# A graph layer's opening: later adjacency loads and gate weights fetched behind the last table write, one product moved behind a transpose, rows normalized a step later

## The chip, the cores and the metric

The kernel runs on one core of a Trainium2 chip. The metric is the device time of one execution in microseconds, the median of several. A profiled execution has its own time; the profile's times count from the first instruction of the span.

## What is computed

Two graph layers on x (3327 x 256, float32) with a sparse 0/1 adjacency adj (3327 x 3327, about four ones in a row), each followed by a residual and a layer norm. The change lies in layer 0, a graph attention whose result goes through a gated recurrent cell:

```python
Wh = h @ W                                   # h is x
e = leaky_relu(Wh @ a[:F] + (Wh @ a[F:]).T, 0.2)
att = softmax(where(adj > 0, e, -9e15), axis=1)
h_prime = att @ Wh
gi = h_prime @ w_ih.T + b_ih                 # i_r, i_z, i_n
gh = h @ w_hh.T + b_hh                       # h_r, h_z, h_n
r, z = sigmoid(i_r + h_r), sigmoid(i_z + h_z)
n = tanh(i_n + r * h_n)
x1 = layernorm(x + (1 - z) * n + z * h)
```

Layer 1 takes x1, builds a dense top-p attention (queries, keys, sorting by thresholds, two steps) beside a walk over adj, and gives the output. It takes most of the time and is not changed.

## The kernel before

Rows are handled in 26 tiles of 128 (NT; the last has 127). Layer 0 never forms the dense attention: it finds the ones of each adj row, gathers the neighbours' rows of Wh from a table in DRAM, and sums them with weights.

**Projection.** `run` first loops over t, the 26 tiles. `project` transposes x on PE (L753), copies on ACT (L754), multiplies by W (L758), copies the result into one of six `table` buffers (L762) and writes it on ACT's DMA queue to the DRAM table `whx` (L763 and L764, the DMA itself in the helper `move_rows`, L102). The next tile's transpose and L754 are issued ahead of this tile's L758 to L764. ACT's queue also carries, between these writes, the loads of adj tiles 1 and 2 (L1084, at t = 4 and 10) and of the gates' weights `whh` and `wih` (L1087, at t = 15 and 17). `totals` closes the stage: a maximum over all tiles and the mean row, written to the table as its last row (L794); `tell_src` splits scores into bfloat16 parts (L776 to L779).

**Searching.** `neighbours` is a generator of five steps for a tile of adj: four `max_index` searches (L819, one for each quarter of the columns, on DVE) and a step of small operations (L824 to L832). It also asks for the load of the adj tile three further on, on SP's queue (L822), since three buffers (`array`) rotate. `find` does one step. Each load goes in two parts, the first three quarters and the last.

**The pipeline of tiles.** `advance` is one phase: some `find` steps, then, every sixth phase (EVERY = 6), the start of a new tile; then each open tile, oldest first, issues its next step; then one step of `first_logits`, which starts layer 1's first scores once all searches are done. Phase 6t + s thus holds step s of tile t. A phase isn't a barrier: PE, ACT, DVE and POOL issue in the order of the program, and each runs on as far as its own waits let it.

```python
        engines = {
            mybir.EngineType.PE, mybir.EngineType.Activation, mybir.EngineType.DVE, mybir.EngineType.Pool,
        }
        with self.tc.manual_schedule(engines=engines):
```

SP is not in the set. [...]

The steps of a tile that matter here:

| step | what | engine, line |
|---|---|---|
| 0 to 2 | degree, its prefix sum `pst` | DVE L851, POOL L858 to L872, PE L865 |
| 4, 7 | mid, y; mem | ACT L875 to L878; DVE L884 |
| 6 | tell | POOL L880, L881 |
| 10, 12 | pe; ei, erow | PE L889, ACT L893 |
| 13 | which, hit, k | DVE L898 to L906 |
| 14 to 17 | edge list; five gathers from `whx`; src, e | POOL L908, L613, L918, L921 |
| 20, 21 | squares | ACT L927 |
| 22 | e | DVE L929 to L931 |
| 23 to 25 | five exponents | ACT L936 |
| 26 | weighted sum acc | PE L940 |
| 28, 29 | rs; h; pn's product of x | DVE L943, ACT L947, PE L950 and L953 |
| 30 | prz's product of x; transposes ph of h | PE L956 and L958, L961 |
| 31 | hT | ACT L964 |
| 33, 34 | products of hT | PE L967, L972 |
| 35 to 38 | gates, n, row statistics | ACT L978, L987; DVE L981 to L994 |
| 39 | power, shift | POOL L996 to L999 |
| 40 | normalized row, its write to `x1_rows` | ACT L1001, L102 |
| 41 on | query and key: ptq, xtq, pq, qT, kT | `qk`, PE L626, L636, ACT L629, L643, L644 |

From t = 13 (EARLY) the projection loop calls `advance` itself, so phases 0 to 12 lie in it; the other phases follow `totals`. The searches in a phase are `min(1, phase % 3)` in the loop, one from phase 13 to 23, and then FINDS = (0, 0, 0, 2, 1, 2) by the phase's place in the six.

Of the kernel before, what the change touches and what calls it, by code (L numbers as in the profile page):

```python
# [9 lines left out]
F32 = mybir.dt.float32  # L10
# [6 lines left out]
P = 128  # L17
N = 3327
D = 256
DC = D // P  # L20
DA = 64
NT = (N + P - 1) // P
# [35 lines left out]
EVERY = 6  # L58

EARLY = 13  # L60

FINDS = (0, 0, 0, 2, 1, 2)
# [19 lines left out]
def rows(t):  # L82
    return TAIL if t == NT - 1 else P


def cols(t):
    return slice(t * P, t * P + rows(t))
# [9 lines left out]
def move_rows(engine, dst, src, r):  # L97

    full = r // 16 * 16
    for a, b in ((0, full), (full, r)):  # L100
        if a < b:
            engine.dma_start(dst[a:b], src[a:b])  # L102
# [545 lines left out]
class Layer0:  # L648
# [165 lines left out]
    def neighbours(self, t):  # L814

        nc, r, ad = self.nc, rows(t), self.ad[t % 3]
        at = self.st.tile([P, SEG, 8], U32, tag="at8", name=f"at8_{t}")
        for g in range(SEG):
            nc.vector.max_index(at[:r, g, :], self.ones8[:r], ad[:r, g, :])  # L819
            yield  # L820
        if t + 3 < NT:
            self.load_adj(t + 3, nc.sync)  # L822
        off = self.st.tile([P, SEG, 8], F32, tag="off", name=f"off{t}")
        nc.vector.tensor_tensor(off[:r], self.base[:r], at[:r], ALU.subtract)  # L824
        key = self.key[:r, t]
        nc.vector.scalar_tensor_tensor(key, at[:r], SW - 0.5, off[:r], ALU.is_lt, ALU.mult)
        info = self.info[:, t]
        flat = key.rearrange("p g e -> p (g e)")
        nc.vector.max(info[:r, :8], flat)
        rest = self.st.tile([P, SEG * 8], F32, tag="rest", name=f"rest{t}")  # L830
        nc.vector.match_replace(rest[:r], info[:r, :8], flat, 0.0)
        nc.vector.max(info[:r, 8:16], rest[:r])  # L832
        yield

    def tile(self, t):

        nc, r, sh = self.nc, rows(t), self.sh
# [4 lines left out]
        def to(step):  # L842
            nonlocal done
            while done < step:
                done += 1
                yield
# [70 lines left out]
        src = self.small("src", f"src{t}", EB)  # L917
# [12 lines left out]
        nc.vector.scalar_tensor_tensor(e, e, ALPHA, e, ALU.mult, ALU.max)  # L930
        nc.vector.tensor_tensor(e[:, 0, :], e[:, 0, :], e[:, 1, :], ALU.subtract)  # L931

        for step, ks in ((23, (0, 1)), (24, (2, 3)), (25, (4,))):
            yield from to(step)
            for k in ks:
                nc.scalar.activation(ms[k], ms[k], AF.Exp, bias=e[:, 0, k : k + 1], scale=-FAR)  # L936
# [12 lines left out]
        ones3 = self.ones3[:, :r]  # L949
        nc.tensor.matmul(pn[:r], ones3, self.bias[:, 2 * D :], start=True, stop=False)  # L950
        xs = [self.xT[:, c, cols(t)] for c in range(DC)]
        for c in range(DC):
            nc.tensor.matmul(pn[:r, :D], xs[c], self.whh[:, c, 2 * D :], start=False, stop=False)  # L953
        yield from to(30)
        prz = self.ps1.tile([P, 2 * D], F32, tag="prz", name=f"prz{t}")
        nc.tensor.matmul(prz[:r], ones3, self.bias[:, : 2 * D], start=True, stop=False)  # L956
        for c in range(DC):
            nc.tensor.matmul(prz[:r], xs[c], self.whh[:, c, : 2 * D], start=False, stop=False)  # L958
        ph = self.ps.tile([P, DC, P], F32, tag="tr", name=f"ph{t}")
        for c in range(DC):  # L960
            nc.tensor.transpose(ph[:, c, :r], h[:r, c * P : (c + 1) * P], sh.ident[:r, :r])  # L961
        yield from to(31)
        hT = self.work.tile([P, DC, P], F32, tag="hT", name=f"hT{t}")
        nc.scalar.copy(hT[:, :, :r], ph[:, :, :r])  # L964
        yield from to(33)
        for c in range(DC):
            nc.tensor.matmul(  # L967
# [29 lines left out]
        nc.gpsimd.tensor_tensor(mv[:r, 1:2], mv[:r, 1:2], self.power[:r], ALU.pow)  # L997
        shift = self.small("shift", f"shift{t}")
        nc.gpsimd.tensor_scalar(shift[:r], mv[:r, 0:1], mv[:r, 1:2], -1.0, ALU.mult, ALU.mult)  # L999
        yield from to(40)  # L1000
        nc.scalar.activation(x1, x1, AF.Identity, bias=shift[:r], scale=mv[:r, 1:2])  # L1001
        move_rows(nc.scalar, sh.x1_rows[t * P : t * P + r, :], x1, r)
        yield from to(41)
        yield from sh.qk(self.ps, self.work, 0, t, x1, "tr")

    def erow(self, t):
# [28 lines left out]
    def run(self):  # L1035
        nc, sh = self.nc, self.sh
        self.load_adj(0, nc.sync)
        parts = self.st.tile([P, 4, DC], F32, tag="parts", name="parts", bufs=1)
        cuts = (0, 8, 16, NT - 2, NT)
        tiles, finding = [], iter(())  # L1040
        found = phase = 0
        self.done, self.searched = 0, False
        logits = self.first_logits()

        def find():

            nonlocal finding, found
            if next(finding, True):
                if found < NT:
                    finding = self.neighbours(found)  # L1050
                    found += 1
                    next(finding)
                else:
                    self.searched = True

        def advance(finds):
            nonlocal phase
            for _ in range(finds):
                find()
            if phase % EVERY == 0 and phase // EVERY < NT:  # L1060
                tiles.append(self.tile(phase // EVERY))
            for g in list(tiles):
                if next(g, True):
                    tiles.remove(g)
                    self.done += 1
            next(logits, None)
            phase += 1
# [5 lines that stand above are left out]
            self.weights()  # L1073
            opened = [self.project(t) for t in range(NT)]
            qk_weights = sh.make_weights(self.work, self.ps)
            pc = self.ps1.tile([1, 512], F32, tag="acc", name="colsum")
            next(opened[0])
            for t in range(NT):
                if t + 1 < NT:
                    next(opened[t + 1])  # L1080
                for _ in opened[t]:
                    pass
                if t in (4, 10):
                    self.load_adj(1 + t // 10, nc.scalar)  # L1084
                if t in (15, 17):
                    w, src = ((self.whh, self.wih)[t // 17], self.gates[t // 17])
                    nc.scalar.dma_start(w, src.rearrange("(c p) d -> p c d", p=P))  # L1087
                if t in (8, 10):
                    next(qk_weights)
                if t + 1 in cuts:  # L1090
                    k = cuts.index(t + 1) - 1
                    self.column_sums(parts[:, k, :], cuts[k], cuts[k + 1])
                if t - 1 in cuts[1:]:
                    k = cuts.index(t - 1) - 1
                    self.mean_terms(pc, parts[:, k, :], k == 0, False)
                if t == EARLY:
                    self.tell_src(0, EARLY)
                if t >= EARLY:
                    advance(min(1, phase % 3))
                elif t >= EARLY - 8:  # L1100
                    find()
            self.totals(pc, parts[:, 3, :])
            self.tell_src(EARLY, NT)
            while phase < EVERY * NT or tiles:
                advance(1 if phase < 4 * EVERY else FINDS[phase % EVERY])
            for _ in logits:
                pass
        full = self.st.tile([P, 3], F32, tag="full", name="full")

        nc.vector.tensor_reduce(full[:, 0:1], self.key.rearrange("p t g e -> p (t g) e")[:, :, 7], AX.X, ALU.max)  # L1110
        nc.vector.tensor_reduce(full[:, 1:2], self.info[:, :, MAXDEG - 1], AX.X, ALU.max)
        end = self.st.tile([P, NT], F32, tag="e0", name="end", bufs=1)
        nc.vector.scalar_tensor_tensor(end, self.deg, 1.0, self.info[:, :, MAXDEG], ALU.max, ALU.add)
        nc.vector.tensor_reduce(full[:, 2:3], end, AX.X, ALU.max)
        nc.vector.tensor_scalar(full[:, 2:3], full[:, 2:3], -float(EB * P), None, ALU.add)
        nc.vector.tensor_reduce(full[:, 0:1], full, AX.X, ALU.max)
        nc.vector.tensor_scalar(sh.bad[:, 0:1], full[:, 0:1], 0.5, None, ALU.is_gt)
        nc.vector.tensor_scalar(sh.rinv, self.deg, 1.0, None, ALU.add)
        nc.vector.reciprocal(sh.rinv, sh.rinv)
# [860 lines left out]
```

## Time and profile before

| what | value |
|---|---|
| median of 3 runs | 1857.93 us (1853.77 to 1858.95) |
| profiled execution, its own time | 1861.15 us |
| its span | 1859.1 us |
| PE, DVE, POOL, ACT busy over the span | 1666.4, 1318.3, 1158.7, 1031.2 us |
| last table write issued | 63.65 us, the mean row 65.52 us |
| first edge list (L908), last one | 68.33 us, 353.40 us |
| last normalization of layer 0 (L1001) | 394.86 us |

Lines of the profile are read so: start and length in us, engine, line of the kernel, operation, what is written from what. In brackets is the idle time before it and what ended it. A row of waits has who waited for whom, the us in total, how often and the longest. A row of a stretch has the busy us of PE, PE's weight loads, DVE, ACT and POOL, each with its number of instructions, then the granted TensorE clock (1 is full), the mean busy share of the DMA engines and GB/s. "q" behind an engine is its queue, which issues DMAs.

### The profile page before, as it was taken

What the parts mean: (1) busy time and instruction counts of PE and PEld (TensorE: products, weight loads), DVE (VectorE), ACT (ScalarE), POOL (GpSimd) and SP (SyncE); (2) the same over time, 40 slices, a digit from 0 to 9 for tenths busy, and PEclk for the clock granted to TensorE, in tenths of its full rate; (3) what the DMA queues carried; (4) which work ended last, traced back from release to release, by engine and by line L of the source; (5) the groups of instructions that cost most, each with busy time, mean ns of one, the idle gap of its engine ahead of it and who ended that gap; (6) DMA issues with size and microseconds to landing.
All of it is one profiled execution on the core that took longest, in us unless ns stands there. A gap on an engine that the chain in (4) does not pass through costs nothing. (4 is left out here: it accounts for less than half of the span.)

```text
span 1859.1 us, 27521 instructions
## 1 busy us (share of the span) xinstructions
PE 1666.4 (90%) x8093; PEld 1221.4 (66%) x8093; DVE 1318.3 (71%) x4095; ACT 1031.2 (55%) x2373; POOL 1158.7 (62%) x1908
## 2 busy tenths in 40 slices
PE   6589999969999999999996999999999988679994
PEld 4355555547777777777774777777777656568873
DVE  5688888456555665655546999999999876585872
ACT  2356666735556555555653555555555446676563
POOL 1578888637886666666654655666666573455754
PEclk9799998979999999999997999999999998889997
DMA  9766664212221111111101111111111120122330
GB/s 313 229 230 212 212 209 119 70 58 76 83 63 43 41 41 40 44 49 46 43 26 40 46 46 49 49 53 55 51 52 49 49 61 20 40 77 89 120 97 29
DMA packets 95099, 154.22 MB, mean 83 GB/s; under 512 B 16471, under 2 KB 68174, under 8 KB 94941
## 3 DMA queue, kind: packets, MB, share of 16 engines
q1 hardware_dynamic: 63818, 86.51, 14.2%
q0 software_dynamic: 20384, 53.28, 11.0%
q10 hardware_dynamic: 10738, 12.58, 2.1%
q8 instruction: 67, 1.10, 0.3%
q14 instruction: 92, 0.75, 0.1%
HBM read 124.65 MB, written 27.75 MB: 82 GB/s over the span
## 5 line engine op out<-in xcount | busy, mean ns | idle before, releaser
L1419 PE MATMUL pav<-xa,at 128*128 128x256 f32 (+2 forms) x1352 | 333.0, 391 | 8.8 <-ACT at L1405 8.8
L1405 ACT COPY at<-pt 128x512 f32<-128x512 f32 (+2 forms) x364 | 192.0, 542 | 262.7 <-PE pt L1403 168.3
L1419 PE MATMUL pav<-x,at 128*128 128x256 f32 (+2 forms) x1352 | 325.7, 385 | 7.9 <-ACT at L1405 7.6
L1419 PEld LDWEIGHTS pav<-xa,at 128*128 128x128 f32 (+2 forms) x1352 | 247.1, 192 | 90.0 <-ACT at L1405 41.8
L1419 PEld LDWEIGHTS pav<-x,at 128*128 128x128 f32 (+2 forms) x1352 | 244.4, 190 | 72.6 <-ACT at L1405 28.5
L1199 ACT COPY array<-pl 128x416 f32<-128x416 f32 (+4 forms) x405 | 183.1, 503 | 182.8 <-PE pl L1196 179.5
L1212 DVE MAX8 cand<-array 128x8 f32<-128x167 f32 (+5 forms) x921 | 239.0, 335 | 48.5 <-ACT array L1199 48.5
L613 POOL DMA_INDIRECT g<-xf_rows,edge x130 | 136.1, 1047 | 160.0 <-PE pxf L1365 127.9
L613 POOL DMA_INDIRECT g<-x_rows,edge x130 | 146.1, 1124 | 103.6 <-PE ptq L626 70.9
L1196 PE MATMUL pl<-kT,qT 64*128 64x416 f32 (+4 forms) x810 | 198.7, 561 | 6.3 <-ACT x L1584 2.7
L1304 DVE TENSOR_TENSOR_SCAN before<-e 128x40 f32<-128x40 f32 (+3 forms) x52 | 14.5, 279 | 227.0 <-ACT e L1297 217.7
L1357 POOL TENSOR_SCALAR m<-col,erow 128x128 f32<-128x128 f32 x260 | 157.0, 618 | 14.4 <-PE pxf L1365 8.0
L613 POOL DMA_INDIRECT g<-whx,edge x130 | 137.6, 1058 | 43.6 <-issue 35.6
L1365 PE MATMUL pxf<-g,m 128*128 128x256 f32 (+1 forms) x520 | 134.7, 408 | 13.2 <-POOL m L1357 6.4
L1365 PEld LDWEIGHTS pxf<-g,m 128*128 128x128 f32 (+1 forms) x520 | 98.6, 199 | 68.8 <-issue 40.7
L1230 DVE MAX8 lst<-cand 128x8 f32<-128x160 f32 (+3 forms) x364 | 114.6, 315 | 9.2 <-issue 0.2
L1403 PE MATMUL pt<-ident,array 128*128 128x128 f32 (+1 forms) x676 | 100.9, 276 | 6.0 <-DVE array L1320 6.0
L819 DVE FIND_INDEX8 at<-ones,array 128x8 uint32<-128x840 f32 (+1 forms) x104 | 105.6, 1027 | 0.0
L1403 PE MATMUL pt<-ident,p 128*128 128x128 f32 (+2 forms) x676 | 100.3, 274 | 4.3 <-DVE p L1320 4.3
L1403 PEld LDWEIGHTS pt<-ident,array 128*128 128x128 f32 (+1 forms) x676 | 84.9, 144 | 24.2 <-PE pxf L1365 7.6
L1403 PEld LDWEIGHTS pt<-ident,p 128*128 128x128 f32 (+2 forms) x676 | 84.7, 144 | 21.6 <-PE pxf L1365 8.0
L1320 DVE SCALAR_TENSOR_TENSOR array<-array,t,array 128x3327 f32<-128x3327 f32 x26 | 96.2, 3699 | 0.5
(467 smaller groups left out, 3321.6 us busy)
## 6 DMA issues: line engine op xcount, KB each, us to landing
array<-in_adj_dram SPq DMA_DIRECT2D x23, 1248.0 KB
array<-in_adj_dram SPq DMA_DIRECT2D x23, 415.5 KB
xf_rows<-xf SPq DMA_DIRECT2D x50, 128.0 KB
xa_rows<-xa SPq DMA_DIRECT2D x50, 128.0 KB
xfs<-xf_rows SPq DMA_DIRECT2D x50, 128.0 KB
whx<-table ACTq DMA_DIRECT2D x25, 129.5 KB
x_rows<-x ACTq DMA_DIRECT2D x25, 128.0 KB
xb_rows<-xb SPq DMA_DIRECT2D x25, 128.0 KB
```

The costliest lines, as they stand in the source:

```text
L613: self.nc.gpsimd.indirect_dma_start(out=dst[:, b, :], out_offset=None, in_=table[:, :], in_offset=bass.IndirectOffsetOnAxis(ap=self.edge[: ...
L819: nc.vector.max_index(at[:r, g, :], self.ones8[:r], ad[:r, g, :])
L1196: nc.tensor.matmul(pl[:r, :w], q[on], self.sh.kT[on, n, s : s + w], start=True, stop=True)
L1199: nc.scalar.copy(l[:r, h * HALF + s : h * HALF + s + w], pl[:r, :w])
L1212: self.nc.vector.max(cand[:r, g * 8 : g * 8 + 8], src[:r, g * group : min(N, (g + 1) * group)])
L1230: nc.vector.max(lst[:r, k : k + 8], cand[:r])
L1320: nc.vector.scalar_tensor_tensor(v.p[:r], v.l[:r, :N], v.t[:r], v.p[:r], ALU.is_ge, ALU.mult, accum_out=sA[:r])
L1357: nc.gpsimd.tensor_scalar(v.m[:, b, :], sh.col1, sh.erow[:, v.at, b : b + 1], None, ALU.is_equal)
L1365: nc.tensor.matmul(acc[:r, :D], v.m[:, b, :r], v.g[:, b, :], start=(b == 0), stop=(b == EB - 1))
L1403: nc.tensor.transpose(pt[: rows(j), j - j0, :r], v.p[:r, cols(j)], self.ident[:r, :r])
L1405: nc.scalar.copy(at[:, :full, :r], pt[:, :full, :r])
L1419: nc.tensor.matmul(v.acc[: v.r, :D], at[:k, j - 4 * g, : v.r], V[:k, j, :], start=(j == 0), stop=(j == NT - 1))
```

## The change

1. `neighbours` no longer loads the adj tile three further on but puts its number on a list `wanted`; `advance` takes one number a phase from it once the phase is past NT - EARLY = 13, and then loads it on SP's queue.
2. Adj tiles 1 and 2 are loaded on ACT's queue at t = 6 and 13 instead of 4 and 10.
3. The gates' weights are loaded behind `totals`, that is behind the last table write, on ACT's queue.
4. Searches: from t = 4 instead of 5; in the loop every second phase instead of two in three; none in phases 13 to 15; two a phase in 16 to 23.
5. The exponents go in two groups (steps 24 and 25) instead of three (23, 24, 25).
6. prz's bias and product of x are issued in step 31 behind the copy hT, not in step 30 ahead of the transposes ph.
7. The normalization and its write move from step 40 to 41, and `qk` from 41 to 42.

```diff
@@ neighbours
         if t + 3 < NT:
-            self.load_adj(t + 3, nc.sync)
+            self.wanted.append(t + 3)
@@ tile
-        for step, ks in ((23, (0, 1)), (24, (2, 3)), (25, (4,))):
+        for step, ks in ((24, (0, 1, 2)), (25, (3, 4))):
...
         yield from to(30)
-        prz = self.ps1.tile([P, 2 * D], F32, tag="prz", name=f"prz{t}")
-        nc.tensor.matmul(prz[:r], ones3, self.bias[:, : 2 * D], start=True, stop=False)
-        for c in range(DC):
-            nc.tensor.matmul(prz[:r], xs[c], self.whh[:, c, : 2 * D], start=False, stop=False)
         ph = self.ps.tile([P, DC, P], F32, tag="tr", name=f"ph{t}")
...
         nc.scalar.copy(hT[:, :, :r], ph[:, :, :r])
+        prz = self.ps1.tile([P, 2 * D], F32, tag="prz", name=f"prz{t}")
+        nc.tensor.matmul(prz[:r], ones3, self.bias[:, : 2 * D], start=True, stop=False)
+        for c in range(DC):
+            nc.tensor.matmul(prz[:r], xs[c], self.whh[:, c, : 2 * D], start=False, stop=False)
         yield from to(33)
...
-        yield from to(40)
+        yield from to(41)
         nc.scalar.activation(x1, x1, AF.Identity, bias=shift[:r], scale=mv[:r, 1:2])
         move_rows(nc.scalar, sh.x1_rows[t * P : t * P + r, :], x1, r)
-        yield from to(41)
+        yield from to(42)
@@ run
-        self.done, self.searched = 0, False
+        self.done, self.searched, self.wanted = 0, False, []
@@ advance
             for _ in range(finds):
                 find()
+            if self.wanted and phase > NT - EARLY:
+                self.load_adj(self.wanted.pop(0), nc.sync)
@@ run
-                if t in (4, 10):
-                    self.load_adj(1 + t // 10, nc.scalar)
-                if t in (15, 17):
-                    w, src = ((self.whh, self.wih)[t // 17], self.gates[t // 17])
-                    nc.scalar.dma_start(w, src.rearrange("(c p) d -> p c d", p=P))
+                if t in (6, 13):
+                    self.load_adj(1 + t // 13, nc.scalar)
...
                 if t >= EARLY:
-                    advance(min(1, phase % 3))
-                elif t >= EARLY - 8:
+                    advance(min(1, phase % 2))
+                elif t >= EARLY - 9:
                     find()
             self.totals(pc, parts[:, 3, :])
+            for w, src in zip((self.whh, self.wih), self.gates):
+                nc.scalar.dma_start(w, src.rearrange("(c p) d -> p c d", p=P))
             self.tell_src(EARLY, NT)
             while phase < EVERY * NT or tiles:
-                advance(1 if phase < 4 * EVERY else FINDS[phase % EVERY])
+                advance(FINDS[phase % EVERY] if phase >= 4 * EVERY else 2 if phase >= 16 else 0)
```

## The prediction

> **What bounds the kernel now.** I read the cores row (1859.1 us, one core), then stretches of time, because all edits lie in layer 0, which ends near 400 us; behind it the program is the same. First the stretches of the opening (busy us of PE, PEld, DVE, ACT, POOL; granted clock; DMA share; GB/s):
>
> ```profile
> 28.00:34.00 6.00, 3.53 (x20) 2.50 (x18) 5.35 (x16) 0.75 (x2) 0.31 (x2) 1.00 1.06 291
> 34.00:40.00 6.00, 2.31 (x8) 1.79 (x9) 0.38 (x3) 1.62 (x5) 0.37 (x2) 0.74 1.04 398
> 40.00:46.00 6.00, 5.85 (x22) 4.40 (x21) 4.94 (x15) 1.92 (x6) 1.67 (x10) 0.69 1.01 392
> 58.00:64.00 6.00, 4.91 (x29) 2.61 (x28) 3.97 (x13) 2.88 (x8) 0.98 (x6) 1.00 0.61 184
> 70.00:80.00 10.00, 0.52 (x11) 0.45 (x11) 9.17 (x30) 2.78 (x10) 7.84 (x18) 0.50 0.92 333
> ```
>
> All DMA engines are full to about 60 us while PE and ACT idle: the projection waits for transfers. ACT's waits from 12 to 66 us say which:
>
> ```profile
> ACT xT L754 <- DMA whx<-table: 6.0, 4, 3.9
> ACT xT L754 <- DMA array<-in_adj_dram: 5.7, 3, 3.7
> ```
>
> The table write is in front of that copy in ACT's queue, and it waits 11.7 us for older transfers. Then the order of the adj loads (DVE, SP, ACT, in three answers of the timeline):
>
> ```profile
> 32.78 1.03 DVE L819 FIND_INDEX8 at<-ones,array 128x8 uint32<-128x840 f32 x1
> ...
> 33.84 0.37 SPq L102 DMA_DIRECT2D array<-in_adj_dram  x1
> ...
> 45.33 0.33 ACTq L102 DMA_DIRECT2D whx<-table  x1
> 45.80 0.39 ACTq L1087 DMA_DIRECT2D whh<-in_whhT_dram  x1
> ```
>
> The load of adj tile 4 is called for behind the write at 45.33, but leaves at 33.84, 30 ns after the third search of tile 1 (32.78 + 1.03) freed its buffer. SP isn't in the ordered engine set; its place in the code doesn't hold it back.
>
> Then a tile in the steady part, on POOL and on DVE:
>
> ```profile
> 202.78 0.20 POOL L908 TENSOR_SCALAR edge<-k 128x5 uint32<-128x5 f32 x1
> ...
> 211.05 1.01 POOL L613 DMA_INDIRECT g<-whx,edge  x1 [0.31 <-issue]
> 212.09 0.21 POOL L918 TENSOR_TENSOR src<-ei 128x5 f32<-128x5 f32 x1
> 212.41 0.76 POOL L921 TENSOR_SCALAR e<-src,dmax 128x5 f32<-128x5 f32 x1
> 213.13 0.43 POOL L880 CAST tell<-info 128x1 bf16<-128x1 f32 x1
> ...
> 214.53 0.20 POOL L908 TENSOR_SCALAR edge<-k 128x5 uint32<-128x5 f32 x1
> ...
> 212.17 0.54 DVE L884 TENSOR_SCALAR mem<-y,square 128x640 bf16<-128x640 f32 x1
> 212.63 0.42 DVE L989 SCALAR_TENSOR_TENSOR n<-rz,n 128x256 f32<-128x256 f32 x1
> 213.09 0.42 DVE L990 TENSOR_TENSOR x<-x,n 128x256 f32<-128x256 f32 x1
> ```
>
> From the first edge list at 68.33 POOL's queue runs without a hole but the 0.3 us of issue behind each gather. It sets 9.8 us a tile first, 11.75 us for the 18 tiles from 108.9 to 320.3. After 354 the last tiles leave every 9.27 us (h at 361.03, 370.30, 379.56), with PE busy without a gap. So what counts is when POOL starts, its time per tile, and PE's sum in the drain.
>
> **The change part by part.** The sum is against the profiled execution (1861.15 us, span 1859.1), 3.2 us above the median of 1857.93; I take the difference off the median.
>
> Transfers in the opening. Adj loads 1 and 2 stay on ACT's queue, two and three projections later; both gate weights (1.57 MB) leave the stage. Loads 3 and 4 are called for at phases 14 and 15, but by the row above they leave once their buffers are searched, near 25 and 35 us, still inside the stage. From 24 us on before the last write: adj 1 to 4 (6.65 MB), half of adj 5 (0.8), 19 writes (2.5): 10 MB at 340 GB/s (mean of the six stretches 22 to 58) is 29 us: 53. The engines alone: write of tile 6 at 23.84, 7 tiles at 1.3 us (17.76, 18.85, 20.18) and 12 at 1.5 (49.79 to 63.28 for tiles 17 to 25 is 13.5/9) end at 51. The same count for before (12.6 MB from 20.5) gives 57.5, where the DMAs fall quiet near 60.5, 3 us later; with fewer loads colliding I add under half of that: last write at 54.7 instead of 63.28, **-8.6**. The transfers still here (adj 3 beside 1, 4 beside 2) leave ACT waits of 2 to 4 us.
>
> Searches (1.03 us each, the fifth step 1.3 of small operations). Before: 16 steps by phase 12, one a phase to 23, 27 in all. After: 15, none in 13 to 15, two a phase from 16, 31 in all. The first edge list loses the search at 66.33 that stands before it in DVE's queue: **-1.0**. DVE then has between the lists of tiles 0 and 1 8 steps, 8.6 us, plus 1.8 of others: 10.4, where POOL takes 10.8. Between those of tiles 1 and 2: 8 more, 11.1 us with e, mem and k, where POOL takes 9.8: what is late there is `which` L898, POOL behind it: 1.3 less the 0.4 in hand, **+0.9**. This needs adj 3 to 5 landed, which the early SP loads give. Gates behind the mean row: 4.6 us at 340 GB/s from about 57; first used at phase 29 (89.4 now, 21 us behind the first edge list); 0. If ACT must wait for an older transfer to issue them, its next work (mid, phase 16) has 3 us; without cover, that wait counts in full.
>
> Normalization (L1001) a step later, its x1_rows DMA with it. ACT waits 43.6 us for POOL's shift in 16 tiles from 125 to 310, with mid, y, rz, h queued behind. All of it lies beside POOL's full queue, so the wait itself is worth 0. The two later users move too: ptq (PE) now stands beside ph, 0 while PE has time to spare (busy 37.6 of 40 us from 200 to 240, so 0.7 us a tile); without it what it waits counts in full. In the drain a phase is no time; the last norm may stand behind a logits copy (0.91): 0 to +1.
>
> prz's x product behind h's transposes: the same five PE instructions. hT's copy comes 2.3 us sooner (prz bias 0.38, x 1.98), where POOL (steady) and PE's sum (drain) set the end: 0. Exponents in two groups (3, 2) instead of three: the same five at 0.4, all still ahead of the product at step 26; 0. The searches end four steps sooner, so two logit pairs (0.97 each) leave the drain: -2 to 0. I take 0 for norm and logits together.
>
> POOL's time per tile. With the norm out of mid's way I expect k, L884, L989 and L990 up to 1 us earlier against POOL. Rows: e and tell take 1.24 us from start to start (212.41 to 213.65) beside these three, but 0.55 (87.45 to 88.00) in tile 1 without them: 0.69 lost each tile. Moved earlier they lie on the fifth gather and on src. The Trainium skill (SBUF — State Buffer, Who interferes with whom) says that a DVE operation in a two-port mode, or with two SBUF inputs, takes a port pair that GpSimd shares, for the whole instruction, and that descriptor generation starves likewise. By it nearly all of the loss would move along (L884's 0.54 to the gather, 0.2 to src): 0. The trace is milder: the gather at 95.91 beside L884 took 1.33 against 1.00 (one at 76.17 only 1.10), so +0.33, +0.2, -0.69: -0.2 a tile, 18 tiles **-3.6**. I take the trace; the ends are -0.6 (all freed: -11) and +0.3 (L985 or L990 on two more POOL operations: +5).
>
> Sum: -8.6 - 1.0 + 0.9 - 3.6 = -12.3; by the rule -8.7. Predicted 1857.93 - 12.3 = 1845.6, about 1846.
>
> **The rivals.** *The likeliest* (0.50): start 8 to 9 us earlier, tile slightly shorter; own range 1840 to 1852. *POOL freed* (0.15): 0.6 less per tile, -8.7 - 11: 1838. For it: nothing but the lock lengthens those two rows. Against: five gathers leave POOL few moments when DVE is harmless. *The lock lands worse* (0.14): +0.3 a tile, -8.7 + 5: 1854. *The opening moves less* (0.13): the change does not do what it says, as SP's loads keep their time, the 11.7 us of ACT waits return behind adj 3 and 4; only the gates' 4.6 us and the search's 1.0 are won, less 0.9 and with no gain per tile: 1853.
>
> *Slower* (0.08): one mechanism, the searches at the head of DVE's queue. If loads 3 to 5 do wait behind the last write, they start with the gates at 52 us: 6.6 MB. At the 144 GB/s of the stretch from 80 to 90 that is 46 us, adj 5 at 98; five steps and tile 6's first follow, near 109 with adj 6, and tile 2's edge list behind them in DVE's queue comes 20 us after its old 88.92: less some 3 won later, 1875. At the 333 GB/s of the stretch from 70 to 80 adj 5 lands at 72 and nothing is lost. It decides where adj 5 lands after about 79. Against it: that stretch had nothing else to move, and SP isn't held.
>
> **How the numbers follow.** What this kernel's measurement can tell from no change is about 0.3%, 5.6 us: faster is under 1852.4. The likeliest and the freed case lie there (0.65), of the two small ones half (0.13): 0.78. The other half, same: 0.13. Slower, with a little of the worse lock: 0.09. The range 1834 to 1856 takes in the ends of the time per tile and leaves out the slow case.
>
> **What would show it.** First L908 near 58.5 (56 to 62) instead of 68.33; adj 3 leaving SP near 25, far ahead of the last table write; the ACT waits on transfers 11.7 down to 2 to 4; L908 to L908 11.75 down to 11.4 to 11.7, by e and tell shorter than 0.76 and 0.43; the wait of L1001 for L999 gone without a gain of its own; h every 9.27 us at the end. I am wrong if POOL waits long for k, if first edge lists stay past 64, or if the gain sits after 400 us.

## The result and the profile after

| what | before | after |
|---|---|---|
| median of 11 runs each | 1858.00 us (1853.77 to 1859.08) | 1849.76 us (1846.67 to 1854.28) |
| span of the profiled execution, its clock | 1859.1 us, 0.951 | 1846.6 us, 0.960 |
| last table write, mean row issued | 63.65, 65.52 us | 63.26, 65.14 us |
| first edge list (L908) | 68.33 us | 66.95 us |
| L908 to L908, steady tiles | 11.75 us | 11.25 us |
| last normalization of layer 0 (L1001) | 394.86 us | 385.01 us |

The ratio after to before is 0.9958, 95% interval 0.9948 to 0.9967. Of the profiled span's 12.5 us, layer 0 holds 9.9; the rest is in layer 1, which is the same program and takes 1461.6 us in this execution and 1464.2 in before's. In the thirteen profiled executions of this document it takes from 1458.9 to 1467.4, so these 2.6 us are within what executions differ by.

First the stretches of the opening, of after (columns as before: PE, PEld, DVE, ACT, POOL; granted clock; DMA share; GB/s):

```profile
28.00:34.00 6.00, 6.00 (x33) 4.13 (x31) 4.80 (x17) 2.32 (x7) 0.56 (x3) 1.00 1.03 396
52.00:58.00 6.00, 1.80 (x16) 1.20 (x16) 2.64 (x7) 1.25 (x6) 0.37 (x2) 0.77 0.92 315
58.00:64.00 6.00, 5.43 (x15) 2.85 (x16) 1.17 (x5) 2.06 (x6) 1.11 (x7) 0.66 0.18 56
```

The projection runs without a gap from 28 to 34 us. But in the stretch from 52 to 58 PE idles beside full DMA engines, and in the next it is busy at a clock of 0.66. The hole has moved, not gone. ACT's waits of after from 12 to 66 us:

```profile
ACT mid L875 <- DMA array<-in_adj_dram: 3.9, 1, 3.9
...
ACT xT L754 <- DMA whx<-table: 3.1, 1, 3.1
...
ACT xT L754 <- DMA array<-in_adj_dram: 2.2, 1, 2.2
```

That is 9.2 us of the old 11.7. (The 3.1 stands beside the load of adj 1, which ACT's own queue issues from 21.98 on, for 2.63 us.) The longest of them in SP's, ACT's and PE's timelines of after; SP's first row is adj tile 3:

```profile
25.02 3.54 SPq L102 DMA_DIRECT2D array<-in_adj_dram  x2
...
50.08 1.80 SPq L102 DMA_DIRECT2D array<-in_adj_dram  x2
```

```profile
53.46 0.38 ACT L762 COPY table<-pw 128x258 f32<-128x258 f32 x1 [0.50 <-PE pw L758]
57.31 0.33 ACTq L102 DMA_DIRECT2D whx<-table  x1
57.69 0.26 ACT L875 ACTIVATE mid<-pst,half 128x1 f32<-128x1 f32 x1 [3.85 <-DMA array<-in_adj_dram]
```

```profile
52.24 1.14 PE L758 MATMUL pw<-W_sb,xT 128*128 128x258 f32 x4 [0.29 <-ACT table L762]
...
58.05 2.09 PE L758 MATMUL pw<-W_sb,xT 128*128 128x258 f32 x4 [3.50 <-ACT info L876]
```

Adj tile 5 leaves SP at 50.08, among the last table writes. The write of tile 23 is ready at 53.84, leaves at 57.31, and mid, which stands behind it in ACT's queue, is put down to the adj load. The write doesn't read that load's data. I read the row as a link between the two queues: the write had to wait until that load had landed. SP's adj loads wait for table writes too, with which they share no data: 30.3 us in five waits in before, from 12 to 66 us. What links them (in my reading a semaphore for landed transfers that the program gives to DMAs of both queues in turn) no run shows. Full DMA engines alone are not enough: in before adj 5 leaves at 49.36, with a DMA share of 1.01 from 52 to 58, and no table write behind it waits. PE pauses 3.5 us, and the product after it takes 2.09 us, where the same product at 52.24 takes 1.14.

Now one steady tile of after, on POOL and on DVE:

```profile
194.72 1.23 POOL L613 DMA_INDIRECT g<-whx,edge  x1 [0.30 <-issue]
195.97 0.21 POOL L918 TENSOR_TENSOR src<-ei 128x5 f32<-128x5 f32 x1
196.29 0.33 POOL L921 TENSOR_SCALAR e<-src,dmax 128x5 f32<-128x5 f32 x1
196.58 0.18 POOL L880 CAST tell<-info 128x1 bf16<-128x1 f32 x1
...
197.73 0.20 POOL L908 TENSOR_SCALAR edge<-k 128x5 uint32<-128x5 f32 x1
```

```profile
194.19 0.54 DVE L884 TENSOR_SCALAR mem<-y,square 128x640 bf16<-128x640 f32 x1
194.65 0.42 DVE L989 SCALAR_TENSOR_TENSOR n<-rz,n 128x256 f32<-128x256 f32 x1
195.11 0.42 DVE L990 TENSOR_TENSOR x<-x,n 128x256 f32<-128x256 f32 x1
```

e fell from 0.76 to 0.33 and tell from 0.43 to 0.18: from the start of e to the start of the operation behind tell it is now 0.56 us instead of 1.24. The three DVE operations, which lay on e and tell before, now end at 195.53, before src begins. The fifth gather under L989 and L990 grew from 1.01 to 1.23.

Why they come earlier is seen on ACT. In before, the normalization stood ahead of mid:

```profile
206.62 0.60 ACT L1001 ACTIVATE x<-x,shift,mv 128x256 f32<-128x256 f32 x1 [1.35 <-POOL shift L999]
...
207.62 0.26 ACT L875 ACTIVATE mid<-pst,half 128x1 f32<-128x1 f32 x1 [0.40 <-ACT x L1001]
```

In after, mid comes first and waits for half, which stands four POOL operations ahead of the first of power and shift:

```profile
199.64 0.26 ACT L875 ACTIVATE mid<-pst,half 128x1 f32<-128x1 f32 x1 [2.62 <-POOL half L868]
...
201.54 0.60 ACT L1001 ACTIVATE x<-x,shift,mv 128x256 f32<-128x256 f32 x1 [0.78 <-POOL shift L999]
```

From that tile's L908 (202.78 before, 197.73 after) mid begins 4.84 us later in before and 1.91 in after; ei (L893), which DVE's `which` needs, 8.14 and 6.54. So L898, k and the three operations behind them start earlier against POOL's fixed sequence. From 125 to 310 us ACT now waits 40.2 us for half and 12.5 for shift (before: 43.6 for shift); as POOL's queue is full, neither costs.

### The profile page after: what moved, and what is told of

Same layout as the page of the kernel before. It is cut to its first block, busy times and chain, and to the rows that moved or that the text cites. A ratio compares the mean times of both kernels' runs of the same rounds, so it can differ in the third digit from the quotient of the medians.

```text
span 1846.6 us, 27541 instructions
## 1 busy us (share of the span) xinstructions
PE 1654.3 (90%) x8093; PEld 1215.7 (66%) x8093; DVE 1314.9 (71%) x4095; ACT 1030.2 (56%) x2373; POOL 1148.5 (62%) x1908
## 3 DMA queue, kind: packets, MB, share of 16 engines
q0 software_dynamic: 20384, 53.28, 10.9%
## 5 line engine op out<-in xcount | busy, mean ns | idle before, releaser
L613 POOL DMA_INDIRECT g<-x_rows,edge x130 | 140.4, 1080 | 103.9 <-PE ptq L626 71.0
L1358 POOL TENSOR_SCALAR m<-col,erow 128x128 f32<-128x128 f32 x260 | 162.6, 639 | 14.6 <-PE pxf L1366 8.0
```

The source lines that it names most:

```text
L613: self.nc.gpsimd.indirect_dma_start(out=dst[:, b, :], out_offset=None, in_=table[:, :], in_offset=bass.IndirectOffsetOnAxis(ap=self.edge[: ...
L1358: nc.gpsimd.tensor_scalar(v.m[:, b, :], sh.col1, sh.erow[:, v.at, b : b + 1], None, ALU.is_equal)
```

## The experiments

**The normalization alone.** Three theories were on the table: (A) the whole gain is the normalization's new place, (B) it is the new places of loads and searches in the opening, (C) it is prz's new place.

```diff
 before:
-        yield from to(40)
+        yield from to(41)
         nc.scalar.activation(x1, x1, AF.Identity, bias=shift[:r], scale=mv[:r, 1:2])
...
-        yield from to(41)
+        yield from to(42)
```

> The kernel before with only the normalization and its row write at step 41 and qk at 42. Theory A (the norm's wait for POOL's shift stood ahead of mid, y, rz and h in ACT's queue and so set when DVE's two-input operations fall on POOL's e and tell): L908 to L908 goes from 11.75 to 11.2 to 11.4 us, e from 0.76 to under 0.45, tell from 0.43 to 0.18; first L908 stays at 68 us; total 7 to 10 us under before. Theory B (the searches' new places in the phases did it): 11.7 us a tile, e and tell as before, total within 2 us. Theory C (the product moved behind the transposes did it): the same as B.

Measured: median 1850.04, ratio 0.9951 (0.9933 to 0.9970); first edge list at 68.53, tiles 11.16 apart, last normalization at 384.69. POOL's rows of this kernel:

```profile
197.21 0.32 POOL L921 TENSOR_SCALAR e<-src,dmax 128x5 f32<-128x5 f32 x1
197.50 0.18 POOL L880 CAST tell<-info 128x1 bf16<-128x1 f32 x1
```

Two changed numbers give the ratio of the whole change. Theory A stands. The tile is even 0.09 us shorter than after's 11.25, or 1.6 us in 18 tiles: in the tile of these rows the fifth gather takes 1.20 and not 1.23, and L870 and L871 take 0.27 and 0.20 and not 0.31 and 0.23. Which of the other items costs this was not tried.

**prz alone** (item 6 of the change; the lines in parentheses stand for the rest).

```diff
 before, steps 30 and 31:
-        (prz: bias, product of x, ahead of ph)
...
         nc.scalar.copy(hT[:, :, :r], ph[:, :, :r])
+        (prz: bias, product of x)
```

> The kernel before with only prz's bias and product of x moved behind hT's copy. Theory A: L908 to L908 stays 11.75 (11.7 to 11.8), the wait of L964 (hT) for ph shrinks from 17 us in the window 125 to 310 to under 5 and nothing follows from it; total within 2 us. Theory C: 11.2 to 11.4 us a tile and 7 to 10 us won.

Measured: one time of 1858.39; tiles 11.72 apart, e 0.75, tell 0.43, last normalization at 397.4 behind a first list at 69.56. hT's wait for ph, 17.0 us in before from 125 to 310, is gone, and the tile is as long as before: theory C falls, and the earlier copy is hidden, as the prediction had it.

**The opening alone** (items 1 to 4; shown as a change of before, shortened).

```diff
 before, with:
+            self.wanted.append(t + 3)      # and its loads from advance
+                if t in (6, 13):           # adj 1, 2
+            (gates' loads behind totals; the new search counts)
```

> The changed loads, gate weights and searches alone; norm, exponents and prz as before. Theory A: tile distance 11.6 to 11.8, first L908 at 67 us (1.4 earlier, as in the changed kernel), total 1 to 3 us under before. Theory B: 11.25 us a tile and 8 to 10 us won in all.

Measured: median 1856.84, ratio 0.999 (0.9979 to 1.0000); last table write 64.68, first list 68.89, tiles 11.69 apart. The four items of the opening are worth nothing that can be measured; theory B falls. The first list at 68.89 beside 66.95 in after comes from the same opening code. Five profiled executions here have it, and their first lists come at 66.95, 68.32, 68.70, 68.89 and 70.48 us; the three with the old opening have 68.33, 68.53 and 69.56. So after's profile is the luckiest of its five, and the 1.4 us of its row are not a gain.

**Adj tile 5 held back.** If the late load of adj 5 makes the hole at 54 to 58, it goes when that load stands on ACT's queue, behind the writes, which is ordered.

```diff
 after:
-                self.load_adj(self.wanted.pop(0), nc.sync)
+                held = self.wanted.pop(0)
+                self.load_adj(held, nc.scalar if held == 5 else nc.sync)
```

> The changed kernel with adj tile 5 alone put on ACT's queue in phase 16, where the program's order holds it behind the last table write; tiles 3 and 4 stay on SP. If the 3.9 us in which ACT waits at 53.5 to 57.3 for adj 5's first part, and the half-speed products behind that pause, are what ate the opening's gain: the last table write at 57 to 58 instead of 63.3, first L908 at 61 to 62 instead of 67.0, all later edge lists as much earlier, total about 5 us under the changed kernel. If the pause only moves (to adj 4, or to the searches of tile 5 at the head of DVE's queue): first L908 earlier by less than 2, or the lists of tiles 2 and 3 back where they were, total within 2 us of the changed kernel.

Measured: median 1845.44 (1839.05 to 1849.12), ratio 0.9913 (0.9887 to 0.9939). Last write 61.05, first list 64.73, every later list 2.2 to 2.8 us ahead of after's profile. The sign is as expected, but the list is some 3 us later than it was to be: two waits of 3.9 us remain, one beside the load of adj 1 (ended at 25.35), one put down to an adj load (ended at 38.57). The late pause of PE is gone:

```profile
58.00:64.00 6.00, 4.38 (x19) 1.85 (x18) 2.41 (x13) 1.96 (x7) 1.21 (x7) 1.00 0.15 46
```

This repeats. In all five executions of the new opening with adj 5 on SP, mid waits 1.4 to 4.7 us for the adj load near 54 to 60 us, PE pauses 1.1 to 4.3 us, the product behind the pause takes 1.5 to 2.1 us, and the clock from 58 to 64 is 0.51 to 0.66. In the four that hold adj 5, or 4 and 5, mid waits 0.4 us, no such product is longer than 1.14 us there, and the clock is 1.00.

**Adj tiles 3, 4 and 5 held back.** The same line with `held <= 5`. Now the change does what its words say.

> The changed kernel with adj tiles 3, 4 and 5 on ACT's queue in phases 14 to 16, so that all three really stay behind the last table write. What the prediction's slow rival says: the searches of tile 3 to 5 stand at the head of DVE's queue for their rows, the edge lists of tiles 1 and 2 come late and the time is at or over that of the changed kernel although the first edge list comes at 54 to 58. If the transfers at the front are the only cost: first L908 at 54 to 58, every later list as much earlier, adj 5 landed by 79, total 8 or more us under the changed kernel.

Measured: median 1851.38, ratio 0.9949 (0.9931 to 0.9967). Last write 54.94 and first list 58.63 are the prediction's 54.7 and 58.5, but that is no proof of its sum, which had adj 3, 4 and half of 5 among the bytes ahead of the last write. But the second list is at 77.83, as in after (77.74). POOL's and DVE's rows of this kernel say why:

```profile
58.63 0.44 POOL L908 TENSOR_SCALAR edge<-k 128x5 uint32<-128x5 f32 x1 [2.83 <-DVE k L906]
...
77.83 0.43 POOL L908 TENSOR_SCALAR edge<-k 128x5 uint32<-128x5 f32 x1 [2.25 <-DVE k L906]
```

```profile
67.02 0.09 DVE L819 MATCH_VALUE_LOAD at<-ones,array 128x8 f32 x1 [8.02 <-DMA array<-in_adj_dram]
```

All loads now start behind the writes, and the searches at the head of DVE's queue wait 8.0 us for them, with k behind. (ACT, which issues these loads, stands still until 67.47 as well, but ei is copied at 68.50, and `which` begins only at 76.77, behind the searches.) The 8.3 us won at the first list are lost by the second: the transfers' time was not hidden, only put elsewhere.

**Adj tiles 4 and 5 held back,** the middle way, with `held in (4, 5)`.

> The changed kernel with adj tiles 4 and 5 on ACT's queue in phases 15 and 16; tile 3 stays on SP and lands early. First L908 at 58 to 62; tile 3's searches find their rows, tile 4's wait little. Expected between the kernel with tile 5 held and one without any of the three loads at the front: 3 to 7 us under the changed kernel in total. If the searches starve already here, lists 1 to 3 lose what the first has won.

Measured: median 1856.58, ratio 0.9973 (0.9964 to 0.9983), which is worse than holding one, and worse than holding three, though the intervals of these two touch. First list 63.06, then 13.4 and 15.6 us to the next two; DVE waits for adj loads 3.64 us at 72.30 and 5.16 at 84.23. The expected gain of some us is a miss: starved searches cost more than the projection won.

**Which DVE operations lengthen POOL's.** If the sharing of ports that the prediction names is the reason for e's 0.76, an operation with two SBUF inputs put onto e must lengthen it, and one with a single input must not. In after a search runs on DVE when e begins. Two kernels add one operation behind L994; its result is not used.

```diff
 after, behind bn_aggr (L994), in the first kernel:
+        nc.vector.tensor_tensor(n[:r], x1, n[:r], ALU.subtract)
 in the second:
+        nc.vector.tensor_reduce(probe[:r], x1, AX.X, ALU.add)
```

> The changed kernel with one more DVE operation a tile behind the row statistics, 128x256, whose two inputs both lie in SBUF (n <- x1 - n, read by nobody; it adds about 0.42 us to DVE). If two-input operations shut POOL's small operations out while they run, it now lies on e and tell: e or tell 0.2 to 0.45 us longer, L908 to L908 11.45 to 11.7 us. If e and tell were long for another reason (DVE's load, ACT's order), both stay at 0.32 and 0.18 and the distance at 11.25.

> The same place, but a reduction of x1 with one input in SBUF, of about the same length. If the number of SBUF inputs decides: e and tell stay at 0.32 and 0.18, L908 to L908 stays at 11.25 (11.2 to 11.3). If any DVE work at this place lengthens them: as with the two-input operation.

With two inputs (DVE and POOL rows):

```profile
188.86 0.39 DVE L995 TENSOR_TENSOR n<-x,n 128x256 f32<-128x256 f32 x1
```

```profile
189.03 0.42 POOL L921 TENSOR_SCALAR e<-src,dmax 128x5 f32<-128x5 f32 x1
```

With one:

```profile
186.26 0.39 DVE L996 TENSOR_REDUCE probe<-x 128x1 f32<-128x256 f32 x1
```

```profile
186.43 0.33 POOL L921 TENSOR_SCALAR e<-src,dmax 128x5 f32<-128x5 f32 x1
```

Both probes begin 0.17 us before e and take 0.39. Beside the first e ends 0.2 us after the probe's end (0.42 long), beside the second it keeps its 0.33. The distance of tiles is 11.30 and 11.24. This holds in every steady tile but one: e takes 0.42 or 0.43 in the first kernel, 0.32 or 0.33 in the second. The shift of 0.09 is smaller than the 0.2 that was expected at least, and the tiles than 11.45: the probe already had 0.17 us behind it when e began. So the time for which DVE is busy doesn't decide. That the number of SBUF inputs does is the nearest reading; the probes also differ in what they write (256 columns and one), and this was not separated.

**After and the held adj 5 again,** side by side.

> The changed kernel itself once more, beside the next two on one chip, as their measure and to see how much the opening differs from one execution to the next: ratio to before 0.995 to 0.997, L908 to L908 11.25 us, first L908 anywhere from 66 to 70.

> The changed kernel with adj tile 5 alone held behind the last table write on ACT's queue, once more. If its first reading (0.9913 to before) holds: 3 to 6 us under the changed kernel of the same call. If that was one chip's luck: within 2 us of it.

Measured: after 1854.02, ratio 0.9960 (0.9945 to 0.9976); with adj 5 held 1849.86, ratio 0.9940 (0.9925 to 0.9954). First lists at 68.70 and 64.81. The 4.2 us between the medians are of the size of the 3.9 between the lists; the intervals just overlap.

**src and e on DVE.** If POOL alone sets the steady tile, work taken off it must shorten the tile. On top of the held adj 5:

```diff
-        nc.gpsimd.tensor_tensor(src, ei[:, :, self.SC], ei[:, :, self.SC3], ALU.add)
+        nc.vector.tensor_tensor(src, ei[:, :, self.SC], ei[:, :, self.SC3], ALU.add)
...
-        nc.gpsimd.tensor_scalar(e[:, 1, :], src, self.dmax, None, ALU.add)
+        nc.vector.tensor_scalar(e[:, 1, :], src, self.dmax, None, ALU.add)
```

> The same with src and e (L918, L921) on DVE instead of POOL. POOL's queue sets the time of a tile: it loses 0.61 us (src to tell, start to start), DVE gets about 0.4. If POOL is the bound: 10.6 to 10.9 us a tile, or about 11.0 if PE (10.9 us of work a tile) takes over, so 4 to 9 us under the kernel with tile 5 held. If DVE or PE bound the tile already: 11.2 or more, no gain.

Measured: median 1833.03 (1830.71 to 1836.53), ratio 0.9855 (0.9837 to 0.9872): the fastest version here, 16.8 us under the held adj 5 beside it, where 4 to 9 were expected. POOL of this kernel at the place of the rows above:

```profile
185.31 1.05 POOL L613 DMA_INDIRECT g<-whx,edge  x1 [0.30 <-issue]
186.37 0.20 POOL L880 CAST tell<-info 128x1 bf16<-128x1 f32 x1
```

tell follows the gather at once. Most tiles are 10.38 us apart, 0.87 less than 11.25: 0.61 for src and e (start of src to start of tell in after, 195.97 to 196.58), 0.18 as this gather takes 1.05 for 1.23, and 0.08 of small gaps. The expected 10.6 to 10.9 had left the gather out; 18 tiles at 0.87 are 15.7 us. No other engine stopped it: the last normalization is at 367.0, where the held adj 5 has 383.0.

## Why the prediction was right, and where a step was not

The forecast was 1846.0 us in a range of 1834 to 1856; the median is 1849.76. The sum said -12.3. Layer 0 gave -9.9 in the profiled executions, the medians differ by 8.2. The total is near by luck: one term was far too large and another too small, and in good part they cancel. In the profiled pair the first list gives -1.4, the searches behind it +0.4 and the steady tiles -8.8 (108.90 to 320.25 before, 107.69 to 310.24 after), together -9.8. Over the three executions with the old opening and the five with the new one the first list gains nothing (middle values 68.53 and 68.70), and 0 + 0.4 - 8.8 = -8.4 is what the medians show.

- **Transfers in the opening, -8.6: the mis-sized step; it measured -0.4 in this profile, and nothing over the five.** The mechanism (ACT's copies and writes behind older transfers) and the time of SP's loads were right: adj 3 left SP at 25.02, well ahead of the last table write. What failed is "with fewer loads colliding I add under half of that" and "ACT waits of 2 to 4 us": the waits came to 9.2. The sum took the bytes at the mean rate (end at 53, the engines alone at 51) and 1.7 us for collisions; but a collision isn't a matter of bytes per us. First lists past 64 were the prediction's own sign that it is wrong here. One adj load, leaving at 50.08 in front of a small write, came with a stop of that write of 3.5 us, and of ACT and PE with it, and PE's clock was low behind the pause. The adj 3, 4, 5 kernel reaches 54.9 once no adj load from SP is in the way. In after they are in the way, which the prediction knew and priced too low.
- **The search ahead of the first list, -1.0:** no search stands ahead of it in any of the five executions. From the last write to the list it is 4.7 us in before and 3.7 in after, but 4.2 to 5.1 in the other four, since DVE waits there 1.0 to 1.3 us for PE at L789 instead of 0.45 (the clock from 62 to 64 is 0.50 in these four, 0.98 in after). The search is gone as forecast, and waits for PE take a part of it back.
- **Two searches a phase, +0.9:** lists of tiles 1 and 2 are 10.20 apart, before 9.81: +0.4, and the same in the other executions with this opening (10.20 to 10.23).
- **POOL's time per tile, -0.2 (-3.6 in 18 tiles): too small; measured -0.5, -8.8 (11.25 us a tile, under the forecast 11.4 to 11.7).** The mechanism is as the prediction put it: the three operations left e and tell (-0.68) for the fifth gather. It was sized with +0.33 on the gather and +0.2 on src. The gather took +0.22, and src kept its 0.21, since L990 ends before it. The end that the prediction gave as -0.6 (POOL freed) was the nearer one. The rule of the Trainium skill (SBUF — State Buffer, Who interferes with whom) was weighed there as moving all of the loss to the gather and to src; the page says that descriptor generation starves beside the two-port modes, and infers that a tensor_tensor leaves it alone. The trace decides for +0.22 on a gather under L989 and L990, neither nothing nor the 0.77 us for which they lie on it. One reason is plain in the rows: L884, the 0.54 us operation, ends at 194.73, just as the gather begins at 194.72, and so falls mostly into the 0.30 us of issue between gathers. For the small operations the probes agree with the page's distinction of one SBUF input and two.
- **The wait of L1001 for L999, worth 0 by itself:** right. It became 12.5 us of the same wait and 40.2 for half, at no cost.
- **prz, hT, exponents, gates, logits, each at 0:** right for prz alone; the others were not tried one by one. In the drain h comes at 338.51, 351.84, 360.26 and 369.53, no longer every 9.27 us, but these three intervals are 31.0 us together as before (30.9).
- **The rivals.** "The opening moves less" held in its first half (SP's loads keep their time, waits return), "POOL freed" in the other; together they are near the forecast. The slow rival's mechanism is real, as the adj 3, 4, 5 kernel shows, but its deciding point was set wrong: "adj 5 lands at 72 and nothing is lost" fails, for loads moving at 370 GB/s from 58 to 68 still cost 8.0 us of DVE's time, as the search at the head of its queue needed one of them. There the loss was as large as the gain at the first list, and no larger.

What stays open: how adj 5's load holds the write, since no run changes that link alone; and what lengthens the fifth gather: with src and e on DVE both L989 and L990 lie on it too, and it takes 1.05, and in after L985, with two SBUF inputs as well, lies on the gather at 192.09, which takes 1.01.

## What to carry to other kernels

Where one engine's queue is full and sets the pace, look at which of its operations last longer beside a neighbour's, and what fixes the neighbour's moment: here the order of two waits in ACT's queue decided it, two lines worth 0.5% against nothing for a reordered opening. A transfer that is moved to a better place in the code must be held by a queue that keeps the order; otherwise it leaves when its buffer is free, and it may stop small writes of another queue, as adj 5's load did here. When transfers do wait, count what the engines will do in the meantime: an earlier first tile is worth nothing if the second waits for the loads.

## What was not expected of the hardware

The product at L758 (four matmuls) took 2.09 us after a pause of PE of 3.5 us, and 1.86 for the next tile, against 1.14 ahead of the pause; the granted clock of that stretch was 0.66. A pause of 2.42 us, before 25.08, was followed by 2.09 us as well. An indirect gather beside DVE operations with two SBUF inputs grew by only 0.22 us (1.01 to 1.23), where e on POOL takes 0.76 instead of 0.33. The same opening code gave first edge lists from 66.95 to 70.48 us in five executions, so one profile can't tell a gain of 1 or 2 us there.
